# A cross-attention kernel in two-level Strassen form: GpSimd's reductions placed ahead of VectorE work on PSUM, one operand sum handed to DMA, one product in blocks in fewer batches

## The chip, the cores and the metric

The kernel runs on one core of a Trainium2 chip. The metric is the device time of one execution in microseconds (us); lower is better. The kernel before took 707.7 us, the median of three runs (703.13 to 709.08). A profile is one further execution, seen through the hardware profiler, with its own time.

The core has a matrix engine (TensorE, "PE" in the profile, with its weight loads as "PEld"), VectorE ("DVE"), ScalarE ("ACT"), GpSimd ("POOL") and SyncE ("SP"), each with an instruction queue worked in order. They meet only by semaphores. DMAs are issued from the queues of SP, ACT and POOL. TensorE writes to PSUM; VectorE and ScalarE reach both PSUM and SBUF.

## The reference

All of it is float32, with 8 batches, C = 512 channels, N = 1024 positions and D = 64:

```python
q = jnp.einsum('bcn,dc->bnd', x1, Wq) + bq
k = jnp.einsum('bcn,dc->bdn', x2, Wk) + bk[:, None]
v = jnp.einsum('bcn,dc->bdn', x2, Wv) + bv[:, None]
attn = jax.nn.softmax(jnp.einsum('bnd,bdm->bnm', q, k), axis=2)
return jnp.einsum('bcm,bnm->bcn', v, attn) + x1
```

Since the rows of `attn` sum to one, the result is Wv · (x2 · attnᵀ) + bv + x1, and so the kernel computes it: first Y = x2 · E with E the exponentials, not yet divided, then Y is divided by the sums, then Wv · Y.

## The kernel before

**Layout.** The scores are held with the key position m on the partitions, in two tiles per batch, `e[0]` and `e[1]`, one for each half h of the queries (512 columns). The softmax runs over m, which means over eight tiles (VectorE folds them, 128x1024 at a time, L249, then the two halves of what is left, L253) and then over the 128 partitions. That last step is GpSimd's `partition_all_reduce`: `highest` (L268) for the maxima, `total` (L272) for the sums. Both read from SBUF what `fold_halves` has just written. The sums then go to HBM and back to be inverted and spread (`invert` with a reciprocal on VectorE at L280, `spread` at L287).

**Seven products instead of eight.** Y is a product of 2 x 2 blocks in Winograd's form of Strassen's algorithm. The left blocks are `a["11"]` to `a["22"]` (x2 transposed, loaded by DMA) with the sums S1 to S4; the right blocks are those of E with the sums T1 to T4. The seven products are numbered 1, 2, 6, 7, 5, 3, 4 in the order in which TensorE does them. Wv · Y is done in the same way, with sums of the weights made once (`w["S1"]` and so on) and sums of Y.

**Two forms of a product of the first stage.** In the plain form (`multiply`, L391) it is 2 x 4 matmuls of 128x512 per product, each seen as two records. In batches 2 to 8 all seven products are done **in blocks**: the same algorithm once more, seven inner products of 2 matmuls of 128x256 (L458, again two records each), for which VectorE first makes inner sums: `inner_left` (four of 128x256, L431) and `inner_right` (one of 128x1024 at L447, two of 128x512 at L450 and L451). What TensorE leaves is put together by ScalarE copies (L467, L495) and by VectorE: `complete` (L501 on PSUM, L535 in SBUF) and `join` (L550, PSUM plus SBUF). Product 6 in blocks needs in addition `reseed`, which writes the joined result back to PSUM (L557) for product 5 to add to.

**Order.** The whole program is one schedule written out by hand (`manual_schedule`): the order of the calls in `period` is the order in each engine's queue. `weave` takes one step of each of several lists in turn. A period handles the first stage of one batch s, the scores of the next batch n (`scores_0`, `scores_and`), and the second stage of s (`second(1)` to `second(4)`), with loads for the batches after (nn, nnn). On TensorE a steady period runs: products 1 and 2, product 6, four score tiles and the next queries, products 5, 7, 3, four score tiles and the next keys, product 4, then the seven products with the weights. While product 2 runs, VectorE folds the sums of half 1, makes the inner sums of product 6, and `total(s, 1)` starts GpSimd as soon as the fold is done; two inner sums of product 6 are still to come then. `highest(n, 0)` comes at the end of `scores_0`, `highest(n, 1)` after the result of product 4 has been taken out by `evict_y(s, "21")`, and `total(n, 0)` near the end, ahead of `evict_o(s, "21")`.

**S4.** The left sum S4 is one VectorE instruction over SBUF (L109, `sum_a(s, "S4")`), written with the opposite sign; `evict_t3` (L567) adds accordingly. S1, S2 and S3 of later batches already come by DMA: a plain load and an accumulating DMA from GpSimd's queue (`begin_s1`/`end_s1`, `add_11`). GpSimd's queue issues every accumulating DMA of the kernel: T3 (`sum_t3`, L340), T4 (`copy_t4`, L334), the sums of the exponentials (`add_tile`, L645), the x1 blocks of the output (L590, L641).

**Batch numbers.** The title counts from 1. The code counts from 0 in `s.b`: batch 3 is `s.b == 2`. Batch 1 (`s.b == 0`) has a schedule of its own.

Of the kernel before, what the change touches and what calls it, by code (L numbers as in the profile page):

```python
# [16 lines left out]
def kernel(  # L17
# [47 lines left out]
    nc = tc.nc  # L65
# [36 lines left out]
    def left_sums(a, *ks):  # L102

        for k in ks:
            if k == "S3":
                nc.vector.tensor_tensor(a["21"], a["11"], a["21"], ALU.subtract)
                a["S3"] = a["21"]
            elif k == "S4":
                nc.vector.scalar_tensor_tensor(a[k], a["12"], -1.0, a["S2"], ALU.mult, ALU.subtract)  # L109
            else:  # L110
                x, y, op = {"S1": ("21", "22", ALU.add), "S2": ("11", "S1", ALU.subtract)}[k]
                nc.vector.tensor_tensor(a[k], a[x], a[y], op)
# [13 lines left out]
    class Batch:  # L126
        def __init__(self, b):
            self.b = b
            self.a, self.e, self.t, self.y, self.o = {}, {}, {}, {}, {}
            self.mx, self.top, self.den, self.few, self.rden, self.row = {}, {}, {}, {}, {}, {}  # L130
            self.tmp, self.bank = {}, {}
            self.inner = {}

# [24 lines left out]
    def end_s1(s):  # L158

        nc.gpsimd.dma_start(s.a["S1"], x2T[s.b, 1, 1], accum_op=ALU.add)  # L160

    def negate(s, k):
# [87 lines left out]

    def fold_halves(s, h, op):
        f = s.mx[h]
        nc.vector.tensor_tensor(f[:, 0, :], f[:, 0, :], f[:, 1, :], op)  # L253

    def folds(s, h, kind, op):

        return [lambda i=i: fold(s, h, i, kind, op) for i in range(1, MH)] + [lambda: fold_halves(s, h, op)]

# [7 lines left out]
    def highest(s, h):  # L266
        s.top[h] = sb.tile([P, H], F32, tag="top", name=f"top_{s.b}_{h}", bufs=2)
        nc.gpsimd.partition_all_reduce(s.top[h], s.mx[h][:, 0, :], P, ReduceOp.max)  # L268

    def total(s, h):  # L270
        s.den[h] = sb.tile([P, H], F32, tag="den", name=f"den_{s.b}_{h}", bufs=2)
        nc.gpsimd.partition_all_reduce(s.den[h], s.mx[h][:, 0, :], P, ReduceOp.add)  # L272
        s.few[h] = sb.tile([P, H // P], F32, tag="few", name=f"few_{s.b}_{h}", bufs=2)
        nc.gpsimd.dma_start(
            s.few[h], s.den[h][0:1, :].rearrange("o (p f) -> o p f", p=P)
        )
# [74 lines left out]
    def sum_e(s, *ks):  # L351
        weave(sums_e(s, *ks))
# [211 lines left out]
    def evict_t3(s):  # L564
        s.y["T3"] = y = sb.tile([P, 2, H], F32, tag="y12", name=f"yT3_{s.b}")
        for j in range(2):
            nc.vector.tensor_tensor(y[:, j, :], s.bank["a", j], s.tmp[7][:, j, :], ALU.add)  # L567

# [5 lines left out]
    RESULT = {"11": ("c", 1), "22": ("c", 5), "12": ("a", None), "21": ("c", 6)}  # L574

    def evict_y(s, k):

        bank, add = RESULT[k]
        s.y[k] = y = sb.tile([P, 2, H], F32, tag=f"y{k}", name=f"y{k}_{s.b}")
        for j in range(2):  # L580
            nc.vector.tensor_tensor(y[:, j, :], s.bank[bank, j], s.tmp[add][:, j, :], ALU.add)

# [206 lines left out]
    def period(s, n, nn, nnn):  # L789

        late = s.b >= 1

        def first(i):
# [19 lines left out]

        def scores_0(*rows):
            then = scores_and(n, 0, 1, "c", next_queries if nn else nothing)
            if late:
                reseed(s)
            weave(folds(n, 0, "max", ALU.max), *rows)
            highest(n, 0)
            return then  # L820
# [11 lines left out]
        if s.b == 0:  # L832
# [3 lines left out]
            sum_e(s, "T1", "T2")  # L836
            fold_halves(s, 0, ALU.add)
            total(s, 0)
# [10 lines left out]
            first(6)  # L849
            scores_0()  # L850
            weave(inner_left(s, 4, s.a["22"], "a12"), inner_right(s, 4, s.t["T4"], "eT2"))
            lefts_3 = inner_left(s, 3, s.a["S4"], "aI3")
# [13 lines left out]
        else:  # L866
            complete_1 = multiply_seeded(s, 1, "y11")
            weave(
                folds(s, 1, "sum", ALU.add),
                [nothing, complete_1] + inner_right(s, 6, s.t["T2"], "yT1", "yT2"),  # L870
                [nothing, nothing] + inner_left(s, 6, s.a["S2"], "i2"),
            )
            total(s, 1)
            invert(s, 0)
            hooks = {5: lambda: copy_u1(s, 0), 4: lambda: copy_u1(s, 1)}
# [3 lines left out]
            complete_2()  # L879
            evict_y(s, "11")  # L880
            sum_t4(s)
            hooks = {6: lambda: copy_t4(s, 0), 5: lambda: copy_t4(s, 2)}
            complete_6, *join_6 = multiply_joined(s, 6, "v", hooks)
            evict_q = None
            if n:
                weave(
                    inner_right(s, 5, s.t["T1"], "y21", "u1"),
                    inner_left(s, 7, s.a["S3"], "yT4"),
                    [nothing, lambda: sum_a(s, "S4")],
                )  # L890
                complete_6()
                weave(join_6)
                evict_q = scores_0(inner_left(s, 5, s.a["S1"], "i2"))
                rights_7 = inner_right(s, 7, s.t["T3"], "yT1", "yT2")
            else:
                weave(
                    inner_left(s, 5, s.a["S1"], "a11"),
                    inner_right(s, 5, s.t["T1"], "y21", "u1"),
                    inner_left(s, 7, s.a["S3"], "yT4"),
                )  # L900
                complete_6()
                weave(join_6)
                reseed(s)
                sum_e(s, "T3")
                rights_7 = inner_right(s, 7, s.t["T3"], "yT1", "yT2")
                rights_7.pop(0)()
                sum_a(s, "S4")
            spread(s, 0)
            shares(s, 1)
            weave(rights_7, inner_left(s, 3, s.a["S4"], "aI3"))  # L910
            complete_5, *join_5 = multiply_joined(s, 5, "r", {6: evict_q} if nn else {})
            complete_5()
            weave(join_5, inner_right(s, 3, s.t["22"], "eT1"))
# [40 lines left out]
        if s.b == 0:  # L954
            weave(tops)
            highest(n, 1)
        hooks = {}
# [12 lines left out]
        if nn:  # L970
            load_a(nn, "21", "22")
        evict_y(s, "21")
        lefts_1 = rights_2 = []
        if late and n:
            if nn:
                tops[2]()
            lefts_1 = inner_left(n, 1, n.a["11"], "i2")
            rights_2 = inner_right(n, 2, n.e[0][:, 1], "eT4")
# [4 lines left out]
        if late and n:  # L983
            if nn is None:
                weave(tops, lefts_1[1:])
                lefts_1 = []
            highest(n, 1)
            add_11(n, "S3")
            weave(rights_2, lefts_1[1:])
# [32 lines left out]
        if n:  # L1022
# [9 lines left out]
            weave(early)  # L1032
            fold_halves(n, 0, ALU.add)
            total(n, 0)
# [44 lines left out]
```

## Time and profile before

| | |
|---|---|
| median of three runs | 707.7 us |
| the three runs | 707.7, 703.13, 709.08 us |
| the profiled execution | 707.89 us, span 706.1 us |
| mean granted clock of TensorE | 0.985 |
| busy, share of the span | PE 96%, DVE 93%, ACT 49%, POOL 31% |

The span goes from the first instruction to the end of the last; what lies around it is 1.8 us here. A busy PE is a PE with a matmul in flight: the records overlap, so the spacing of their starts tells the rate, 0.43 us for 128x512 and 0.22 us for 128x256 at the full clock. In a timeline line the columns are start, length, engine, line of the code, operation, output and inputs, shapes and count, and in brackets the idle time before with what ended it. In the list of waits a line reads "engine, tile, line <- what it waited for: us in total, times, longest".

### The profile page before, as it was taken

What the parts mean: (1) busy time and instruction counts of PE and PEld (TensorE: products, weight loads), DVE (VectorE), ACT (ScalarE), POOL (GpSimd) and SP (SyncE); (2) the same over time, 40 slices, a digit from 0 to 9 for tenths busy, and PEclk for the clock granted to TensorE, in tenths of its full rate; (3) what the DMA queues carried; (4) which work ended last, traced back from release to release, by engine and by line L of the source; (5) the groups of instructions that cost most, each with busy time, mean ns of one, the idle gap of its engine ahead of it and who ended that gap; (6) DMA issues with size and microseconds to landing.
All of it is one profiled execution on the core that took longest, in us unless ns stands there. A gap on an engine that the chain in (4) does not pass through costs nothing.

```text
span 706.1 us, 7562 instructions
## 1 busy us (share of the span) xinstructions
PE 675.8 (96%) x2528; PEld 423.8 (60%) x2528; DVE 656.3 (93%) x853; ACT 348.5 (49%) x605; POOL 221.9 (31%) x182
## 2 busy tenths in 40 slices
PE   9999999799999999999999999989999989996997
PEld 5333555666557664658547575466754757465863
DVE  1999998999999999999999999999999999999984
ACT  2733455456455564464754555535555547443320
POOL 0133215520445114441144401753034621353000
PEclk9999999899999999999999999998999999999999
DMA  9666479794996929967499857988579772499103
GB/s 305 246 242 237 89 239 161 199 219 122 252 237 176 270 77 291 231 158 247 124 268 232 181 163 204 214 209 188 156 179 192 183 152 39 97 207 282 41 1 119
DMA packets 50774, 131.11 MB, mean 186 GB/s; under 512 B 5552, under 2 KB 7856, under 8 KB 50736
## 3 DMA queue, kind: packets, MB, share of 16 engines
q0 software_dynamic: 22464, 54.60, 42.3%
q1 hardware_dynamic: 27984, 75.64, 29.8%
q8 instruction: 20, 0.33, 0.2%
q10 hardware_dynamic: 288, 0.39, 0.2%
q14 instruction: 18, 0.15, 0.1%
HBM read 87.30 MB, written 16.81 MB: 147 GB/s over the span
## 4 chain that ended last, share of the span: by engine, by line
PE 57%; DVE 26%; DMA 8%; issue 5%; POOL 2%; ACT 1%; SPq 1%; DVEq 0%; POOLq 0%; ACTq 0%
PE ps_ya L458 8%; PE ps_oa L391 6%; PE ps_yc L458 5%; DMA sum<-e 5%; DVE aI L431 4%; PE ps_s L229 4%; DVE eT L315 4%; DVE sum L249 4%; PE ps_q L182 3%; PE ps_i3chain L458 3%; PE ps_oc L391 3%; PE ps_o L411 3%; PE ps_i5chain L458 3%; PE ps_i4chain L458 3%; PE ps_i7chain L458 3%
## 5 line engine op out<-in xcount | busy, mean ns | idle before, releaser
L272 POOL PARTITION_ALL_REDUCE den<-sum x16 | 55.1, 3446 | 80.1 <-DVE sum L253 75.2
L268 POOL PARTITION_ALL_REDUCE top<-max x16 | 39.2, 2450 | 122.6 <-DVE max L253 104.1
L302 DVE TENSOR_TENSOR e<-e,top 128x1024 f32<-128x1024 f32 x60 | 69.9, 1216 | 1.7 <-POOL top L268 1.7
L645 POOL DMA_DIRECT2D sum<-e x21 | 28.5, 1356 | 122.0 <-ACT sum L650 51.5
L306 ACT ACTIVATE e<-e 128x1024 f32<-128x1024 f32 x60 | 61.9, 1057 | 5.8 <-DVE e L302 5.2
L391 PE MATMUL ps_oa<-yT,w_S 128*128 128x512 f32 x128 | 57.5, 592 | 0.0
L391 PE MATMUL ps_oc<-yT,w 128*128 128x512 f32 x128 | 57.4, 592 | 0.0
L238 ACT COPY e<-ps_s 128x1024 f32<-128x1024 f32 x46 | 45.7, 1032 | 13.7 <-issue 7.8
L229 PE MATMUL ps_s<-q,k 64*128 64x512 f32 x188 | 47.3, 608 | 0.9 <-ACT q L671 0.8
L391 PEld LDWEIGHTS ps_oa<-yT,w_S 128*128 128x128 f32 x128 | 24.3, 190 | 30.6 <-issue 30.6
L391 PEld LDWEIGHTS ps_oc<-yT,w 128*128 128x128 f32 x128 | 24.3, 190 | 30.6 <-issue 29.4
L249 DVE TENSOR_TENSOR max<-max,e 128x1024 f32<-128x1024 f32 x30 | 36.6, 1220 | 0.5
L402 ACT COPY uo<-ps_oa 128x512 f32<-128x512 f32 x32 | 18.7, 585 | 35.1 <-PE ps_oa L391 35.1
L458 PE MATMUL ps_i6chain<-eI6yT,aI 128*128 128x256 f32 x56 | 19.0, 473 | 16.7 <-DVE aI L431 16.7
L431 DVE TENSOR_TENSOR aI<-aS 128x256 f32<-128x256 f32 x44 | 32.6, 741 | 0.0
L495 ACT COPY ps_ya<-ps_i1chain 128x256 f32<-128x256 f32 x28 | 10.0, 357 | 41.2 <-PE ps_i1chain L458 37.7
L229 PEld LDWEIGHTS ps_s<-q,k 64*128 64x128 f32 x188 | 16.7, 186 | 22.2 <-issue 15.4
L391 PE MATMUL ps_oa<-y,w_S 128*128 128x512 f32 (+1 forms) x68 | 28.8, 567 | 0.0
L391 PE MATMUL ps_o<-y,w 128*128 128x512 f32 x64 | 28.8, 592 | 0.0
L411 PE MATMUL ps_o<-y,w 128*128 128x512 f32 x64 | 28.8, 592 | 0.0
L572 DVE TENSOR_TENSOR y<-y,den 128x1024 f32<-128x1024 f32 x24 | 28.6, 1220 | 0.1
L431 DVE TENSOR_TENSOR aI<-a 128x256 f32<-128x256 f32 x58 | 27.5, 476 | 0.0
(217 smaller groups left out, 1698.7 us busy)
## 6 DMA issues: line engine op xcount, KB each, us to landing
x_in_x_dram<-in_x_dram SPq DMA_DIRECT2D x60, 512.0 KB, 6.0
a<-in_x2T_dram SPq DMA_DIRECT2D x32, 512.0 KB, 8.0
sum<-e POOLq DMA_DIRECT2D x21, 512.0 KB, 8.7
aS<-in_x2T_dram POOLq DMA_DIRECT2D x14, 512.0 KB, 8.0
uo<-in_x_dram POOLq DMA_DIRECT2D x14, 512.0 KB, 10.5
r<-in_x_dram POOLq DMA_DIRECT2D x14, 512.0 KB, 11.2
out_dram<-r SPq DMA_DIRECT2D x14, 512.0 KB, 4.7
eT<-eT POOLq DMA_DIRECT2D x14, 512.0 KB, 8.4
```

The source lines that it names most:

```text
L229: nc.tensor.matmul(ps[g], s.k[r, ts(i, P)], s.q[r, ts(h, H)], start=True, stop=True)
L238: nc.scalar.copy(e[:, :, i, :], whole)
L249: nc.vector.tensor_tensor(f, e[:, :, 0, :] if i == 1 else f, e[:, :, i, :], op)
L268: nc.gpsimd.partition_all_reduce(s.top[h], s.mx[h][:, 0, :], P, ReduceOp.max)
L272: nc.gpsimd.partition_all_reduce(s.den[h], s.mx[h][:, 0, :], P, ReduceOp.add)
L302: nc.vector.tensor_tensor(e, e, top, ALU.subtract)
L306: nc.scalar.activation(e, e, AF.Exp)
L391: nc.tensor.matmul(ps[:, n], left[ka][:, k, ts(j, P)], right[kb][:, k, n], start=opens and k == 0, stop=i in (2, 3, 4) and k == n_k - 1, s ...
L411: nc.tensor.matmul(ps, w["11"][:, k, ts(j, P)], s.y["11"][:, k, :], start=k == 0, stop=False, skip_group_check=True)
L431: return lambda: nc.vector.tensor_tensor(v[k], v[x], v[y], op)
L458: nc.tensor.matmul(ps, s.inner[i][ka][:, k, :], s.inner[i, "t"][kb][:, k, :], start=opens and k == 0, stop=z in (2, 3, 4) and k == MH // 2 ...
L572: nc.vector.tensor_tensor(s.y[k], s.y[k], rden, ALU.mult)
```

## The change

1. **`fold_halves` for sums** writes to a tile of its own, `half`, instead of in place; the last fold of the halves is taken out of the list that `folds` returns and is called by name. `total` now calls it itself.
2. **`total(s, 1)`** then comes after all inner sums of product 6, and what follows it on VectorE is `complete_2` and `evict_y(s, "11")`, both on PSUM. `invert(s, 0)`, which stood behind `total(s, 1)`, moves behind them.
3. **`highest(n, 0)`** moves from `scores_0` to behind the completion of product 5. `spread(s, 0)` and `shares(s, 1)` (GpSimd's DMAs and a reciprocal) stay behind it, and behind them `join_5` on PSUM.
4. **`highest(n, 1)`** of batches 2 to 6: the fold before it moves between the two halves of `evict_y(s, "21")`, which read PSUM.
5. **S4** of batches 2 to 8: a load from SyncE's queue (`begin_s4`) and an accumulating DMA from GpSimd's (`end_s4`) that adds S2. The sign turns, `evict_t3` subtracts. In batch 1 it stays a VectorE instruction.
6. **Product 6 in blocks** only where `six` holds: `s.b` 2, 3, 4, 5 and 7, which is batches 3 to 6 and 8. Batches 2 and 7 do it in the plain form, `first(6)`, without its inner sums, completion, joins and `reseed`. The order in which the inner sums of products 5, 7 and 3 are woven changes a little everywhere.

```diff
@@ left_sums @@
-            elif k == "S4":
-                nc.vector.scalar_tensor_tensor(a[k], a["12"], -1.0, a["S2"], ALU.mult, ALU.subtract)
             else:
-                x, y, op = {"S1": ("21", "22", ALU.add), "S2": ("11", "S1", ALU.subtract)}[k]
+                x, y, op = {
+                    "S1": ("21", "22", ALU.add),
+                    "S2": ("11", "S1", ALU.subtract),
+                    "S4": ("12", "S2", ALU.add),
+                }[k]
...
+    def begin_s4(s):
+
+        s.a["S4"] = sb.tile([P, MH, C // 2], F32, tag="aS4", name=f"aS4_{s.b}")
+        nc.sync.dma_start(s.a["S4"], x2T[s.b, 0, 1])
+
+    def end_s4(s):
+
+        nc.gpsimd.dma_start(s.a["S4"], s.a["S2"], accum_op=ALU.add)
...
     def fold_halves(s, h, op):
+
         f = s.mx[h]
-        nc.vector.tensor_tensor(f[:, 0, :], f[:, 0, :], f[:, 1, :], op)
+        s.half[h] = f[:, 0, :]
+        if op == ALU.add:
+            s.half[h] = sb.tile([P, H], F32, tag="top", name=f"half_{s.b}_{h}", bufs=2)
+        nc.vector.tensor_tensor(s.half[h], f[:, 0, :], f[:, 1, :], op)
 
     def folds(s, h, kind, op):
 
-        return [lambda i=i: fold(s, h, i, kind, op) for i in range(1, MH)] + [lambda: fold_halves(s, h, op)]
+        return [lambda i=i: fold(s, h, i, kind, op) for i in range(1, MH)]
...
     def total(s, h):
+        fold_halves(s, h, ALU.add)
...
     def evict_t3(s):
...
-            nc.vector.tensor_tensor(y[:, j, :], s.bank["a", j], s.tmp[7][:, j, :], ALU.add)
+            nc.vector.tensor_tensor(y[:, j, :], s.tmp[7][:, j, :], s.bank["a", j], ALU.subtract)
...
@@ period @@
         late = s.b >= 1
+        six = late and (n is None or s.b >= 2 and nn is not None)
...
             complete_1 = multiply_seeded(s, 1, "y11")
-            weave(
-                folds(s, 1, "sum", ALU.add),
-                [nothing, complete_1] + inner_right(s, 6, s.t["T2"], "yT1", "yT2"),
-                [nothing, nothing] + inner_left(s, 6, s.a["S2"], "i2"),
-            )
+            adds = folds(s, 1, "sum", ALU.add)
+            if six:
+                weave(
+                    adds,
+                    [nothing, complete_1] + inner_right(s, 6, s.t["T2"], "yT1", "yT2"),
+                    [nothing, nothing] + inner_left(s, 6, s.a["S2"], "i2"),
+                )
+            else:
+                weave(adds, [nothing, complete_1] + inner_left(s, 7, s.a["S3"], "yT4"))
             total(s, 1)
-            invert(s, 0)
...
             complete_2()
             evict_y(s, "11")
+            invert(s, 0)
+            begin_s4(s)
+            end_s4(s)
             sum_t4(s)
...
-                    [nothing, lambda: sum_a(s, "S4")],
...
-                evict_q = scores_0(inner_left(s, 5, s.a["S1"], "i2"))
...
+                if n:
+                    evict_q = scores_0()
+                    weave(inner_left(s, 5, s.a["S1"], "i2"))
+                    weave(folds(n, 0, "max", ALU.max))
+                else:
+                    reseed(s)
+                    sum_e(s, "T3")
             else:
...
+                copy_t4(s, 0)
+                copy_t4(s, 2)
+                first(6)
+                weave(inner_right(s, 5, s.t["T1"], "y21", "u1"), inner_left(s, 5, s.a["S1"], "i2"))
+                evict_q = scores_0()
+                weave(folds(n, 0, "max", ALU.max))
+            rights_7 = inner_right(s, 7, s.t["T3"], "yT1", "yT2")
+            weave(rights_7, [nothing, nothing] + inner_left(s, 3, s.a["S4"], "aI3"))
+            complete_5, *join_5 = multiply_joined(s, 5, "r", {6: evict_q} if nn else {})
+            complete_5()
+            if n:
+                fold_halves(n, 0, ALU.max)
+                highest(n, 0)
             spread(s, 0)
             shares(s, 1)
-            weave(rights_7, inner_left(s, 3, s.a["S4"], "aI3"))
-            complete_5, *join_5 = multiply_joined(s, 5, "r", {6: evict_q} if nn else {})
-            complete_5()
             weave(join_5, inner_right(s, 3, s.t["22"], "eT1"))
...
-        evict_y(s, "21")
+        if late and nn:
+            steps = evictions_y(s, "21")
+            steps[0]()
+            fold_halves(n, 1, ALU.max)
+            steps[1]()
+        else:
+            evict_y(s, "21")
```

`evictions_y` returns the two VectorE instructions of `evict_y` as a list. The remaining lines of the diff put the calls of `fold_halves` where the lists used to bring them.

## The prediction

> **What bounds the kernel.** I read the page's shares first: TensorE and VectorE are both nearly full, so the question is which of them waits for the other, and where.
>
> ```profile
> PE 675.8 (96%) x2528; PEld 423.8 (60%) x2528; DVE 656.3 (93%) x853; ACT 348.5 (49%) x605; POOL 221.9 (31%) x182
> ```
>
> The list of waits for TensorE and its weight loads has one large place, the inner products of product 6, waiting for VectorE's inner left sums (L431), once in each of batches 2 to 8:
>
> ```profile
> PE ps_i6chain L458 <- DVE aI L431: 16.7, 7, 3.4
> PEld ps_i6chain L458 <- issue: 19.3, 7, 3.8
> ```
>
> The timelines of batch 3 around it, TensorE, VectorE and GpSimd in turn, show why the sum is late:
>
> ```profile
> 220.71 1.03 PE L458 MATMUL ps_i6third<-eI6yT,aI 128*128 128x256 f32 x4
> 223.40 1.10 PE L458 MATMUL ps_i6chain<-eI6yT,aI 128*128 128x256 f32 x4 [1.67 <-DVE aI L431]
> ...
> 218.66 0.68 DVE L253 TENSOR_TENSOR sum<-sum 128x512 f32<-128x512 f32 x1
> 219.26 0.68 DVE L450 TENSOR_TENSOR eI6yT<-eI6yT,eT 128x512 f32<-128x512 f32 x1
> 219.86 2.46 DVE L431 TENSOR_TENSOR aI<-aS 128x256 f32<-128x256 f32 x1
> 222.25 0.68 DVE L451 TENSOR_TENSOR eI6yT<-eT,eI6yT 128x512 f32<-128x512 f32 x1
> 222.85 0.87 DVE L431 TENSOR_TENSOR aI<-aS,aI 128x256 f32<-128x256 f32 x2
> ...
> 219.44 3.59 POOL L272 PARTITION_ALL_REDUCE den<-sum  x1 [5.49 <-DVE sum L253]
> ```
>
> An inner sum that takes 0.41 us elsewhere takes 2.46 us beside GpSimd's reduction: VectorE is held for 2.05 us. Another reduction of the same batch begins ahead of work on PSUM:
>
> ```profile
> 209.64 1.40 DVE L637 SCALAR_TENSOR_TENSOR o<-ps_oc,bv_sb,uo 128x512 f32<-128x512 f32 x2
> 210.96 2.18 DVE L315 TENSOR_TENSOR eT<-eT,e 128x1024 f32<-128x1024 f32 x1
> ...
> 209.83 3.23 POOL L272 PARTITION_ALL_REDUCE den<-sum  x1 [3.14 <-DVE sum L253]
> ```
>
> The two instructions on PSUM keep their 0.74 us each; the SBUF one behind them (1.22 us undisturbed) ends at 213.14, as if released at about 212.0. So a sum holds VectorE's two-input SBUF work until about 2.2 us after its start. A maximum does so for about 1.0 us (237.55 to 238.55: the L447 instruction beside it takes 1.98 instead of 1.22).
>
> The rest of TensorE's time in batch 3 is matmul against matmul: successive starts show no other gap. So a period of 83.2 us is 81.4 us of TensorE and 1.83 us of product 6 waiting. In batches 2, 6 and 8 the wait reaches 3.3 to 3.6 us, and then the matmuls behind it come 0.43 us apart instead of 0.22:
>
> ```profile
> core 0: us, PE busy (x) PEld busy (x) DVE busy (x) ACT busy (x) POOL busy (x), PEclk, DMA share, GB/s
> 137.00:142.00 5.00, 3.87 (x9) 3.18 (x10) 4.93 (x11) 1.32 (x2) 3.81 (x6) 0.50 0.26 43
> ```
>
> The granted clock (PEclk) is 0.50 there, which costs another 2 to 3 us.
>
> **The change, part by part.**
>
> *Product 6, batches 3 to 6.* The fold (0.60) and the hold (2.05) go from in front of the inner sum S2 (the first of the last pair, ended at 223.2). It is then ready at 223.2 - 2.05 - 0.60 = 220.6. TensorE wants it at 220.71 + 0.86 = 221.57, so the wait goes, with 1.0 us to spare. Batches 3, 4, 5: 3 x 1.83 = 5.5 us. Batch 6 takes from 469.49 to 481.98 for product 6, 12.5 us, where gapless it takes 6.2 (28 starts at 0.216 and the change of stage): 6.3 us lost. Its VectorE was 1.5 us late, because one accumulation of sums took 12.2 us to land (427.24 to 439.48) instead of about 7.5. I leave a 0.3 us wait: 6.0.
>
> *Product 6 plain, batches 2 and 7.* 16 records at 0.429 us are 6.87 us against 6.05: 0.82 us more on TensorE, while VectorE is rid of one 128x1024, two 128x512 and four 128x256 sums, a completion and two joins (1.14 + 1.20 + 1.36 + 0.60 + 1.20 = 5.5 us). Its operands are on time: T2 ends at 127.8 in batch 2, S2 lands at 126.2, TensorE asks at 131.77. Batch 2 went from 131.77 to 144.81, 13.04 us; now 6.97: 6.1 saved. Batch 7 also waited 3.65 us in product 5 (568 to 574), since VectorE was behind. From 557.01 to the start of product 7 at 578.56 it took 21.55; plain product 6, scores and product 5 back to back are 6.97 + 3.55 + 6.15 = 16.67: 4.9 saved.
>
> *Batch 8* is bound by VectorE from 629.4, where the last accumulation lands, until product 6 is joined and reseeded (TensorE goes on at 653.84). Only the hold counts: 2.05 less what is left of it (below) = 1.5. TensorE then idles about as long in product 5 as it did in both places together.
>
> *Where the holds go.* Behind `total(s, 1)` come L501 and two L581 (0.60 + 1.20 us on PSUM) and the reciprocal, then an L447 on SBUF: of 2.2 us some 0.3 to 0.5 are left. `highest(n, 0)`: 0.6 us of `join_5` covers part of 1.0, and 0.5 is left of 0.76. `highest(n, 1)`: the fold ends 0.60 earlier, the second L581 covers 0.6, and the scaling of y21 behind it is held for 0.55, where 0.85 fell on an inner sum nobody was waiting for. That scaling ended at 273.04 and now ends at about 273.6, against `second(2)` at 273.80, which needs it. This is the tightest margin. Completion of product 4 waited for ScalarE at 266.09, so VectorE cannot run ahead there. I count 0.2 us in each of five batches: -1.0.
>
> The Trainium skill ("SBUF — State Buffer", Who interferes with whom) says that a VectorE instruction with two SBUF inputs and a GpSimd instruction that reads SBUF exclude each other, for the whole instruction. The first half the rows bear out, the second they don't: the record is 3.23 us, the hold 2.2. With a hold as long as the record, 1.4 instead of 0.4 us would be left after `total(s, 1)` and the y21 scaling would miss `second(2)` by up to 1.5 us: five batches, 7.5 us, a time near 692.
>
> *S4.* VectorE is rid of 1.22 us (L109, off TensorE's path once product 6 is on time: nothing by itself). In its place come a SyncE load and an accumulating DMA, two GpSimd queue entries' worth of order. In batch 3 the buffer is free at 220, when product 2 ends. The nearest rows:
>
> ```profile
> aS<-in_x2T_dram SPq DMA_DIRECT2D x7, 512.0 KB, 7.9
> sum<-e POOLq DMA_DIRECT2D x21, 512.0 KB, 8.7
> eT<-eT POOLq DMA_DIRECT2D x14, 512.0 KB, 8.4
> ```
>
> Loaded by 228, issued on GpSimd (1.3 us), added behind T3's two accumulations, which land about 2.7 us apart: S4 lands near 236, or at 239 if the loads of x2, which start at 235 now and at 233 then, slow it. (The DMA share is 0.34 from 219 to 227, and 1.06 from 227 to 235 while T3 and T4 are added.) GpSimd waits for the load with T4's accumulations, the row DMA of sums and the maximum behind it: T4 lands near 241 instead of 237.4 and is wanted at 255; the maximum is not ready to start before 241. VectorE reaches the sums of S4 near 238, TensorE needs S4 at 245.6. T3 is queued behind the later `total` and lands about 1.1 us later (233.1), just ahead of L447's need near 234.5. Cost of the two DMAs: between nothing and, at the longest landing seen (12.2 us each), S4 at 246; I take nothing, since the medians are four times nearer. The denominators go out some 4 us later and are back by 254 at worst, wanted at 257.
>
> *Plus or minus nothing:* the sign in `evict_t3` (same shape, 0.68), the separate `half` tile (its buffer is last read long before), S4 of batch 1 as an ordinary sum.
>
> **Sum.** 5.5 + 6.0 + 6.1 + 4.9 + 1.5 - 1.0 = 23.0 us off 707.9 (span 706.1 and 1.8 around it), which makes 685. The profiled time is the median. The run at 703.1 fits one without batch 6's late landing (4.4 us): it may be missing before, and costs little after.
>
> **Rivals.**
>
> 1. *Another thing is late (19%).* The accumulated sums of the exponentials landed only 1.3 us ahead of VectorE in batch 3, and behind it in batches 2, 6 and 8. If they, T3 or y21 make TensorE wait about 1.5 us in each of six batches, 9 us come back: 694. For it: the DMA queues carry 1 MB more each period. Against: S4 goes out while product 6 to 5 run, 40 us ahead of those sums, and VectorE gains 3 us a period.
> 2. *The PSUM work is held too (5%).* Then the change doesn't do what it says, and the 2.05 us fall on L501. The inner sums of product 6 are still out before it, so TensorE loses little: 687. Against: L637 at 0.74.
> 3. *Slower: S4 comes late (7%).* VectorE stands at the sums of S4 in order, with product 5's completion, the maximum and product 3's sums behind it. About 3 us of slack lie there. If S4 lands at 244 or later instead of 236, TensorE stands 3.4 us, or less with a clock drop, in each of seven batches, and the gain of 23 is gone; at 248 each batch loses near 7 with the drop: 710 to 735, say 720. For it: GpSimd's order, the DMA share of 1.06 and the 12.2 us landing. Against: the medians.
> 4. *No difference (3%):* the saved time turns up as waits in the second stage.
>
> **Chances.** Forecast 66%, 681 to 689. Faster by over 1% (about what a measurement of this kernel can tell): 0.66 + 0.19 + 0.05 = 0.90; same 0.03; slower 0.07. The range reaches down to 680 (batch 8 without its clock drop) and up to 695, which takes in rivals 1 and 2.
>
> **What would show it.** L431 at 0.42 beside every `total`, no wait of product 6 in batches 3 to 7, a period of 81.4 us, no granted clock of 0.5 but in batch 8; VectorE idle for 2 to 3 us a period. It would be wrong if TensorE waits at `second(2)` for y21, or product 3 for S4, or if the last accumulation lands later against product 6.

## The result, and the profile after

The kernel after takes 684.94 us (median of 4 runs, 684.15 to 686.32) against 705.41 us for the kernel before on the same chip (4 runs, 702.35 to 709.08). The ratio is 0.971, with a 95% interval from 0.965 to 0.977. The forecast was 685.0. The profiled execution took 684.92 us, with a span of 683.1 us and a mean granted clock of 0.997 (before: 707.89, 706.1 and 0.985).

The first part of the page of the kernel after, busy time and share of the span for each engine:

```profile
PE 669.0 (98%) x2504; PEld 415.0 (61%) x2504; DVE 625.4 (92%) x826; ACT 345.8 (51%) x595; POOL 217.7 (32%) x189
```

TensorE has 24 matmul records fewer and is busy 7 us less; VectorE is rid of 27 instructions and 31 us. Of the seven waits of product 6 (16.7 us in all) those of batches 2 to 7 are gone from TensorE's list of waits after. What is left of it, with the longest wait of product 5, lies in batch 8:

```profile
PE ps_i5chain L474 <- ACT d L483: 4.8, 1, 4.8
PE ps_i6third L474 <- DVE aI L447: 1.5, 1, 1.5
...
PE ps_i6chain L474 <- DVE aI L447: 0.8, 1, 0.8
```

The line numbers have moved: the inner left sum L431 is L447 now, the first inner right sum L447 is L463, and the completion L501 is L517. The timelines of batch 3 in the kernel after, TensorE, VectorE and GpSimd in turn, answer those shown of before:

```profile
215.05 1.03 PE L474 MATMUL ps_i6third<-eI6yT,aI 128*128 128x256 f32 x4
215.91 1.03 PE L474 MATMUL ps_i6chain<-eI6yT,aI 128*128 128x256 f32 x4
...
214.52 0.88 DVE L447 TENSOR_TENSOR aI<-aS,aI 128x256 f32<-128x256 f32 x2
215.32 0.68 DVE L268 TENSOR_TENSOR half<-sum 128x512 f32<-128x512 f32 x1
215.92 0.69 DVE L517 TENSOR_TENSOR ps_yc<-ps_yc,v 128x512 f32<-128x512 f32 x1
216.52 1.28 DVE L597 TENSOR_TENSOR y<-ps_yc,uy 128x512 f32<-128x512 f32 x2
217.72 0.16 DVE L296 RECIPROCAL few<-few 128x4 f32<-128x4 f32 x1
217.83 1.58 DVE L463 TENSOR_TENSOR eI5y<-eT 128x1024 f32<-128x1024 f32 x1
...
216.11 3.22 POOL L288 PARTITION_ALL_REDUCE den<-half  x1 [7.82 <-DVE half L268]
```

The second inner product (one line of four records) starts 0.86 us after the first, with no gap. The last inner sums of product 6 come before the fold now. Beside the reduction (216.11 to 219.33) the instructions on PSUM keep their lengths, 0.69 us and 1.28 for a pair, and the reciprocal takes 0.16; only the SBUF instruction behind them is long, 1.58 instead of 1.22. The 0.36 us too many say that it could run from 218.19: the hold ends 2.08 us after the reduction's start, though its record goes on to 3.22.

Cut by batches, from the start of one product 1 to the next (to the end of the span in batch 8), the 23 us are here; batch 1 has got 0.43 us longer:

| batch | before | after | gain | forecast |
|---|---|---|---|---|
| 2 | 88.08 | 81.99 | 6.09 | 6.1 |
| 3, 4, 5, each | 83.21 | 81.17 | 2.04 to 2.06 | 1.83 |
| 6 | 87.52 | 81.17 | 6.35 | 6.0 |
| 7 | 80.41 | 76.51 | 3.90 | 4.9 |
| 8 | 80.75 | 79.87 | 0.88 | 1.5 |
| y21, second(2) | | | 0 | -1.0 |
| sum, with batch 1 | | | 22.9 | 23.0 |

The half clock of batch 2 is gone with its wait. Windows of the kernel after, the first over the same stretch as before and the second over product 5 of batch 8, where TensorE restarts after 4.77 us:

```profile
core 0: us, PE busy (x) PEld busy (x) DVE busy (x) ACT busy (x) POOL busy (x), PEclk, DMA share, GB/s
137.00:142.00 5.00, 5.00 (x20) 2.11 (x20) 3.60 (x7) 2.19 (x4) 4.41 (x8) 1.00 0.69 176
...
632.00:640.00 8.00, 8.00 (x34) 6.85 (x33) 7.48 (x14) 2.00 (x6) 1.95 (x3) 0.86 1.05 191
```

### The profile page after: what moved, and what is told of

Same layout as the page of the kernel before. It is cut to its first block, busy times and chain, and to the rows that moved or that the text cites. A ratio compares the mean times of both kernels' runs of the same rounds, so it can differ in the third digit from the quotient of the medians.

```text
span 683.1 us, 7499 instructions
## 1 busy us (share of the span) xinstructions
PE 669.0 (98%) x2504; PEld 415.0 (61%) x2504; DVE 625.4 (92%) x826; ACT 345.8 (51%) x595; POOL 217.7 (32%) x189
## 4 chain that ended last, share of the span: by engine, by line
PE 93%; DVE 4%; DMA 1%; ACT 1%; issue 1%; SPq 0%; DVEq 0%; ACTq 0%
PE ps_oa L407 12%; PE ps_ya L474 10%; PE ps_oc L407 8%; PE ps_yc L474 8%; PE ps_s L240 6%; PE ps_ya L407 5%; PE ps_o L407 4%; PE ps_o L427 4%; PE ps_q L193 4%; PE ps_k L193 3%; PE ps_i4chain L474 3%; PE ps_i3chain L474 3%; PE ps_i5chain L474 3%; PE ps_i7chain L474 3%; PE ps_i1chain L474 3%; PE ps_i2chain L474 2%
## 5 line engine op out<-in xcount | busy, mean ns | idle before, releaser
L288 POOL PARTITION_ALL_REDUCE den<-half x16 | 51.6, 3225 | 91.2 <-DVE half L268 91.2
L283 POOL PARTITION_ALL_REDUCE top<-max x16 | 31.7, 1980 | 131.3 <-DVE few L296 58.2
L588 DVE TENSOR_TENSOR y<-y,den 128x1024 f32<-128x1024 f32 x24 | 30.4, 1293 | 0.3
L407 PE MATMUL ps_ya<-eT,aS 128*128 128x512 f32 x64 | 28.3, 595 | 0.0
L193 PE MATMUL ps_k<-x_in_x_dram,wqk_sb 128*64 128x512 f32 x112 | 26.0, 600 | 0.4 <-DMA x_in_x_dram<-in_x_dram 0.4
L331 DVE TENSOR_TENSOR eT<-eT,e 128x1024 f32<-128x1024 f32 x16 | 26.1, 1637 | 0.0
```

Of the source, the lines that this page charges most:

```text
L193: nc.tensor.matmul(ps[r, :], w_sb[:, c, :], s.x[:, c, ts(h, H)], start=(c == 0), stop=(c == CT - 1),)
L283: nc.gpsimd.partition_all_reduce(s.top[h], s.half[h], P, ReduceOp.max)
L288: nc.gpsimd.partition_all_reduce(s.den[h], s.half[h], P, ReduceOp.add)
L407: nc.tensor.matmul(ps[:, n], left[ka][:, k, ts(j, P)], right[kb][:, k, n], start=opens and k == 0, stop=i in (2, 3, 4) and k == n_k - 1, s ...
L588: nc.vector.tensor_tensor(s.y[k], s.y[k], rden, ALU.mult)
```

## The experiments

The kernel before took a median of 704 to 711 us in the different sets, so each experiment is read by its ratio to the before of its own set, and by its trace. Differences in us to the kernel after are between medians of different sets, and where they are small the traces decide.

### The place of the sum over the partitions

**e1: the sum of half 1 moved, nothing else.** From the kernel before:

```diff
-                folds(s, 1, "sum", ALU.add),
+                folds(s, 1, "sum", ALU.add)[:3],
...
+            fold_halves(s, 1, ALU.add)
             total(s, 1)
-            invert(s, 0)
...
             evict_y(s, "11")
+            invert(s, 0)
```

> The kernel before with one edit: the sum over the partitions of half 1 starts behind the inner sums of product 6 (fold in place, as before), and the reciprocal of half 0 behind the result of product 1. S4, the maxima and product 6 in blocks stay. Theory (product 6 waited for an inner sum that GpSimd's reduction held up): no wait of product 6 in batches 3 to 6, periods of 81.4 us; batch 2 keeps about 2 of its 7 us, batches 7 and 8 gain 1 to 1.7 each as VectorE bounds them: 688 to 691 us. Rival (VectorE is simply too full, and what counts is that S4 and two product-6 preparations leave it): 700 us or more.

Measured: 692.41 us, ratio 0.982 (0.979 to 0.985). That is 14.0 us of the 20.5 that the whole change brought in its own set. It is 1.4 us more than the top of what the theory gave, and far from the rival's 700. In batches 3 to 5 the wait of product 6 is gone, but a period is 81.47 us and not 81.17: product 5 takes 6.45 us to product 7 instead of 6.15. In batches 2 and 6 product 5 loses about 1 us, and in batch 7 it takes 12.36 us to product 7. In batches 2, 6 and 7 TensorE now waits for the inner left sums of product 5 (4.4 us in all), so VectorE is behind there. It has S4 and more inner sums to make than in the kernel after; which of them is to blame this run does not tell.

**e2: the sum of half 1 left out.** From the kernel before:

```diff
-        nc.gpsimd.partition_all_reduce(s.den[h], s.mx[h][:, 0, :], P, ReduceOp.add)
+        whole = s.b == 0 or h == 0
+        if whole:
+            nc.gpsimd.partition_all_reduce(s.den[h], s.mx[h][:, 0, :], P, ReduceOp.add)
...
-            s.few[h], s.den[h][0:1, :].rearrange("o (p f) -> o p f", p=P)
+            s.few[h], (s.den[h] if whole else s.mx[h][:, 0, :])[0:1, :].rearrange("o (p f) -> o p f", p=P)
```

> The kernel before without GpSimd's sum over the partitions of half 1 in batches 2 to 8 (the first partition's partial sums are taken as if they were the total, so half of each output is divided by the wrong numbers); the fold and the inner sums stay in their old order. Theory: the inner sum takes 0.42 instead of 2.46 us, is ready 0.4 us before TensorE asks, and the wait of 1.83 us goes: 687 to 691 us. Rival (the place of the fold among the inner sums is what delays them, not the reduction): the wait stays at 1.2 us or more, 700 us or more.

Measured: 689.98 us, ratio 0.979 (0.975 to 0.982). The fold is still in its old place, ahead of the inner sums, and without the reduction the wait of product 6 is gone in batches 3 to 6 (periods of 81.17 to 81.27 us). The timelines of batch 3 of this kernel, TensorE and VectorE (L433 is L431 of the kernel before):

```profile
217.71 1.03 PE L460 MATMUL ps_i6chain<-eI6yT,aI 128*128 128x256 f32 x4
...
216.00 0.42 DVE L433 TENSOR_TENSOR aI<-aS 128x256 f32<-128x256 f32 x1
```

The inner sum that took 2.46 us takes 0.42. So it was the reduction that made product 6 wait; the 0.60 us of the fold alone do not.

**e3: the sum of half 1 put back early, in the kernel after.**

```diff
-            adds = folds(s, 1, "sum", ALU.add)
+            adds = folds(s, 1, "sum", ALU.add) + [lambda: total(s, 1)]
...
-            total(s, 1)
```

> The changed kernel with the fold and the sum of half 1 back in their old place among the inner sums. Theory: the inner sum for product 6 comes 2.65 us later, 1.0 us were to spare, so 1.7 us of waiting return in each of batches 3 to 6 and some 1.2 in batch 8, nothing in batches 2 and 7 where product 6 is plain: 692 to 694 us. Rival (VectorE has enough room now without S4): 685 to 687 us.

Measured: 692.36 us, ratio 0.981 (0.978 to 0.985). The old picture is back in batch 3; the timelines of this kernel, TensorE, VectorE, GpSimd:

```profile
217.10 1.10 PE L474 MATMUL ps_i6chain<-eI6yT,aI 128*128 128x256 f32 x4 [1.67 <-DVE aI L447]
...
213.55 2.47 DVE L447 TENSOR_TENSOR aI<-aS 128x256 f32<-128x256 f32 x1
...
213.14 3.59 POOL L288 PARTITION_ALL_REDUCE den<-half  x1 [5.49 <-DVE half L268]
```

An inner sum of 0.42 us takes 2.47, TensorE stands 1.67 us, and a period is 83.08 us. Batch 8 loses 1.4. Batches 2 and 7 lose nothing, because in the plain form no inner sum of product 6 stands behind the reduction. The same edit is worth 14.0 us in the kernel before (e1) and 7.4 here. By the traces the difference lies in batches 2 and 6: it gains 3.8 and 4.8 us there, and nothing and 1.9 here. In batch 2 the two edits remove the same wait.

### Product 6 plain

**e6: product 6 in blocks in batches 2 and 7 too.** From the kernel after:

```diff
-        six = late and (n is None or s.b >= 2 and nn is not None)
+        six = late
```

> The changed kernel with product 6 in blocks in batches 2 and 7 as well. Theory: 0.82 us of TensorE saved twice, against waits of 1 + 1.7 us in batch 2, whose last accumulation lands late, and 1 to 3 us in batch 7, where VectorE bounds product 5: 686 to 689 us. Rival (the plain form is the larger part of the gain, as the batches' own gains of 6.1 and 3.9 us suggest): 693 to 696 us.

Measured: 686.88 us, ratio 0.973 (0.968 to 0.978), 1.9 us above the kernel after. Batch 2 goes from 81.99 to 83.38 us and batch 7 from 76.51 to 77.51. So of the 6.1 and 3.9 us that these batches gained, the plain form itself gives 1.4 and 1.0 once the other edits are there; the rest those edits give without it.

### The maxima

**e5: both maxima in their old places.** From the kernel after:

```diff
-                    weave(inner_left(s, 5, s.a["S1"], "i2"))
-                    weave(folds(n, 0, "max", ALU.max))
+                    weave(
+                        folds(n, 0, "max", ALU.max) + [lambda: fold_halves(n, 0, ALU.max)],
+                        inner_left(s, 5, s.a["S1"], "i2"),
+                    )
+                    highest(n, 0)
...
+                fold_halves(n, 0, ALU.max)
+                highest(n, 0)
...
-            if n:
-                fold_halves(n, 0, ALU.max)
-                highest(n, 0)
...
-            steps = evictions_y(s, "21")
-            steps[0]()
+            evict_y(s, "21")
             fold_halves(n, 1, ALU.max)
-            steps[1]()
```

> The changed kernel with both maxima over the partitions back in their old places (half 0 straight behind its folds, half 1 behind both parts of the result of product 4). Theory (TensorE sets the period; the holds of 0.8 us each fall on sums nobody waits for): 684.5 to 686 us. Rival (each hold of VectorE is paid): 0.5 us twice in six batches, 690 us.

Measured: 685.64 us, ratio 0.971 (0.967 to 0.975). The difference of 0.7 us to the kernel after is within what the runs tell apart. The maxima hold VectorE for a shorter time than the sums, and in batches 2 to 6 their old places cost TensorE nothing that the trace shows. (Batch 5 of the profiled execution is 1.0 us longer, but there VectorE stood 1.20 us for an accumulating DMA.) Batch 7 is 0.4 us longer, between the scores and product 4. The timelines of the kernel after show what is left of their holds, VectorE, TensorE and GpSimd:

```profile
235.22 1.63 DVE L463 TENSOR_TENSOR eI3eT<-e 128x1024 f32<-128x1024 f32 x1
...
264.32 1.58 DVE L588 TENSOR_TENSOR y<-y,den 128x1024 f32<-128x1024 f32 x1
...
266.10 1.45 PE L407 MATMUL ps_o<-y,w 128*128 128x512 f32 x3
...
234.74 1.78 POOL L283 PARTITION_ALL_REDUCE top<-max  x1 [9.56 <-DVE few L296]
...
263.78 1.78 POOL L283 PARTITION_ALL_REDUCE top<-max  x1 [2.45 <-DVE max L268]
```

Against 1.22 us undisturbed, the two SBUF instructions are 0.41 and 0.36 us too long, so the holds end 0.89 and 0.90 us after the reductions' starts. The scaling of y21 ends at 265.90, and `second(2)` starts at 266.10 without a wait.

### S4 by DMA

**e4: S4 on VectorE again.** From the kernel after:

```diff
-            begin_s4(s)
-            end_s4(s)
...
+                    [nothing, lambda: sum_a(s, "S4")],
...
```

> The changed kernel with S4 made by VectorE again (one sum of 128x1024 in each of batches 2 to 8, woven into the inner sums of product 5 as before), no DMAs for it. Theory (TensorE sets the period, VectorE has 2 to 3 us of room): 685 to 686.5 us, the one possible loss being 1.1 us in batch 8, which VectorE bounds. Rival (VectorE sets the period): 1.2 us in each of seven batches, 693 us.

Measured: 689.07 us, ratio 0.977 (0.974 to 0.980): neither the theory's 685 to 686.5 nor the rival's 693. Product 6 still waits for nothing in batches 2 to 6. The loss is in the scores' second half: from its first tile to product 4 it takes 7.75 us instead of 7.22 in batches 3 to 5 and 8.08 in batch 6, and batch 8 is 0.84 us longer: 3.3 us by these, of 3.4 in the spans. Of the kernel with S4 on VectorE, the tile of scores on bank a (its list of what it waited for: us, times), then the timelines of TensorE's weight loads and of VectorE:

```profile
  DVE yT L583: 4.1, 10
...
247.61 0.35 PEld L240 LDWEIGHTS ps_sa<-q,k 64*128 64x128 f32 x2 [0.50 <-DVE yT L583]
248.21 0.18 PEld L240 LDWEIGHTS ps_sa<-q,k 64*128 64x128 f32 x1 [0.24 <-DVE yT L583]
...
246.88 1.27 DVE L583 TENSOR_TENSOR yT<-uy,ps_ya 128x512 f32<-128x512 f32 x2
```

The same in the kernel after, where the list has 0.7 us, and the weight loads run through:

```profile
  DVE yT L583: 0.7, 2
...
247.26 0.62 PEld L240 LDWEIGHTS ps_sa<-q,k 64*128 64x128 f32 x4 [0.23 <-issue]
...
245.53 0.70 DVE L517 TENSOR_TENSOR ps_ya<-ps_ya,v 128x512 f32<-128x512 f32 x1 [0.42 <-ACT ps_ya L511]
246.14 1.28 DVE L583 TENSOR_TENSOR yT<-uy,ps_ya 128x512 f32<-128x512 f32 x2
```

The subtraction of `evict_t3` (L583) takes the result of product 3 out of bank a of PSUM, in two halves, and a score tile is written to bank a next. In the kernel after VectorE has 0.42 us of idle time ahead of it. The first half of the bank is free at 246.82, 0.44 us before the tile's weights are loaded at 247.26, and the second half at 247.42, 0.27 us before its weights at 247.69. So there is room for some 0.9 us ahead of the first half and 0.7 ahead of the second. The 1.21 us of S4 are more than that; what is over comes to 0.3 to 0.5 us, and the period loses 0.53. VectorE is not short of time over the whole period: later in the same batch of e4 it still stands idle for 0.36 and 0.75 us.

**e10: the same, with the score tile on bank a put last** instead of third. From e4:

```diff
-            scores_and(n, 1, 2, "a", nothing)
+            scores_and(n, 1, 3 if s.b else 2, "a", nothing)
```

> The kernel after with S4 on VectorE again, and of the scores' second halves the tile on bank a put last instead of third (batches 2 to 7). Theory: what S4 on VectorE cost (689.07 against about 685 us) is that the subtraction that empties bank a comes some 0.8 us later and the score tile on bank a waits for it; with that tile one place (0.86 us) later the wait for this reason is gone from the list of waits. The tile that takes its place waits for ScalarE's copy of an earlier tile instead, an estimated 0.35 us, so the time is 686 to 688.5 us. Rival: VectorE is simply short of 0.5 us in every period, the wait turns up at another instruction on VectorE's results, and the time stays at 689 us or above.

Measured: 689.25 us, ratio 0.968 (0.965 to 0.972). By the time, which is that of e4, it is the rival that came true. By the trace, the wait for bank a is gone from its list, as the theory had it, and in its place TensorE waits for ScalarE's copy of an earlier tile. The timeline of TensorE in batch 3 of this kernel:

```profile
248.48 1.13 PE L240 MATMUL ps_s<-q,k 64*128 64x512 f32 x4 [0.26 <-ACT e L249]
```

The step between two starts is 0.84 us there instead of 0.43. The run alone cannot tell what would have happened without that new wait.

**e11: that order of the tiles alone,** in the kernel after with S4 by DMA. The diff is that of e10.

> The kernel after with S4 by DMA, as it is, and only the order of the score tiles changed as in the run before: the tile on bank a last instead of third. It prices that order by itself. Theory (what S4 on VectorE cost is the wait for bank a, and with the other order the same time went to the wait for ScalarE's copy): that order alone costs the 0.41 us of ScalarE's wait in each of batches 2 to 7, scores to product 4 takes about 7.6 to 7.75 instead of 7.22 us, and the time is 687 to 688.5 us. Rival (the order costs nothing, and VectorE was short of 0.5 us wherever the tile stood): 685 to 685.7 us.

Measured: 687.12 us, ratio 0.975 (0.972 to 0.978), as the theory had it. The order costs 7.74 us from scores to product 4 in place of 7.22 by itself. With it, the periods of batches 3 to 6 are 81.69 or 81.70 us whether S4 is on VectorE (e10) or comes by DMA (e11); of the 1.75 us between the two spans 1.2 are in batch 8 and 0.5 ahead of batch 2. So in a period that ScalarE makes 0.5 us longer, S4 on VectorE costs nothing more. This does not show that bank a was the only place short of time, since the longer period gives VectorE more room everywhere; for bank a speak the waits in the trace of e4.

**e8: S4's accumulating DMA behind T4's two** on GpSimd's queue. From the kernel after:

```diff
             begin_s4(s)
-            end_s4(s)
             sum_t4(s)
...
+                end_s4(s)
                 complete_6()
                 weave(join_6)
...
                 copy_t4(s, 0)
                 copy_t4(s, 2)
+                end_s4(s)
                 first(6)
```

> The changed kernel with the accumulating DMA of S4 issued behind the two of T4 on GpSimd's queue instead of ahead of them. In batch 3 S4 then lands near 239 instead of 230.5 us, where VectorE asks at 231.8 and TensorE at 239.7. Theory (there are about 3 us of slack behind VectorE's wait, as the prediction reckoned): product 3 waits 3 to 4 us for its inner sums in each of batches 2 to 7, with a half clock behind some: 703 to 718 us. Rival (the DMA has ample room): 685 to 688 us.

Measured: 719.11 us, ratio 1.018 (1.014 to 1.023), slower than before and just above what the theory gave. Its timelines in batch 3, VectorE and TensorE:

```profile
243.94 0.76 DVE L447 TENSOR_TENSOR aI<-aS 128x256 f32<-128x256 f32 x2 [6.97 <-DMA aS<-aS]
...
249.19 2.05 PE L474 MATMUL ps_i3third<-eI3eT,aI 128*128 128x256 f32 x4 [3.32 <-DVE eI3eT L463]
251.02 1.91 PE L474 MATMUL ps_i3chain<-eI3eT,aI 128*128 128x256 f32 x4
```

S4 lands at 243.92; measured from product 1 of the batch that is 8.3 us later than in the kernel after. VectorE stands 6.97 us, TensorE 3.32, and then an inner product of four records takes 1.7 to 1.8 us from start to start instead of 0.86. The batch is 87.79 us long, 6.6 more than after: half for the wait and half for the slower clock of TensorE.

### Batch 8

**e7: product 6 plain in batch 8 too.** From the kernel after:

```diff
-        six = late and (n is None or s.b >= 2 and nn is not None)
+        six = s.b >= 2 and nn is not None
...
-                evict_q = scores_0()
-                weave(folds(n, 0, "max", ALU.max))
+                if n:
+                    evict_q = scores_0()
+                    weave(folds(n, 0, "max", ALU.max))
+                else:
+                    sum_e(s, "T3")
```

> The changed kernel with product 6 plain in batch 8 too. Theory: batch 8 has no more waiting for inner sums of product 6 (1.7 + 0.9 us), for the reseeding (4.9 us), nor the half clock behind it (1 us), and pays 0.82 us: product 7 starts 8 us earlier, 676 to 679 us. Rival (batch 8 is bound by VectorE or by the loads of x1 and S4 anyway, and the wait comes back in products 7 to 4): 682 to 686 us.

Measured: 682.96 us, ratio 0.967 (0.963 to 0.971), as the rival had it. Product 7 starts 8.5 us earlier after product 1, and then product 3 waits for S4. Its timelines, VectorE and TensorE:

```profile
636.25 0.76 DVE L447 TENSOR_TENSOR aI<-aS 128x256 f32<-128x256 f32 x2 [6.60 <-DMA aS<-aS]
...
640.47 1.62 PE L474 MATMUL ps_i3third<-eI3eT,aI 128*128 128x256 f32 x4 [3.08 <-DVE eI3eT L463]
```

The load of S4 stands behind four loads of x1 on SyncE's queue: issued at 621.17 and landed at 630.70, where in batch 3 of the kernel after it took 3.6 us.

**e9: the loads of x1 behind that of S4.** From e7:

```diff
-        if n is None:
-            load_x(s, x1)
...
             begin_s4(s)
+            if n is None:
+                load_x(s, x1)
             end_s4(s)
```

> The kernel with product 6 plain in batch 8 too, and in batch 8 the four loads of x1 issued behind the load of S4 instead of ahead of it. Theory: in the run before this one the load of S4 stood behind four loads of x1 on SyncE's queue (issued 621.17, landed 630.70 us) and product 3 waited 1.27 + 3.24 us for S4, at half clock behind that; with the load first, S4 lands some 4 to 9 us earlier, product 3 waits for nothing, and the time is 676 to 678 us. Rival: VectorE, or the x1 blocks that come later now, bound batch 8 all the same, and the time stays at 681 to 683 us, with the wait of product 3 moved to another instruction.

Measured: 679.76 us, ratio 0.955 (0.951 to 0.959) to a before that took 711.24 in this set; batch 8 is 75.34 us instead of 77.95 in e7. The time lies between the two expectations. The load landed 6.1 us earlier, at 624.60, but the accumulation, issued at 625.18, took 7.9 us more. VectorE stood 3.61 us for it, and TensorE still waits. Its timeline of TensorE:

```profile
637.37 1.10 PE L474 MATMUL ps_i3third<-eI3eT,aI 128*128 128x256 f32 x4 [1.67 <-DVE eI3eT L463]
```

**e12: S4 of batch 8 alone on VectorE,** where it had stood idle. From e7, with the loads of x1 in the place of S4's:

```diff
-        if n is None:
-            load_x(s, x1)
...
-            begin_s4(s)
-            end_s4(s)
+            if n:
+                begin_s4(s)
+                end_s4(s)
+            else:
+                load_x(s, x1)
...
             rights_7 = inner_right(s, 7, s.t["T3"], "yT1", "yT2")
+            if n is None:
+                weave(rights_7)
+                rights_7 = []
+                sum_a(s, "S4")
```

> Product 6 plain in batch 8 too, and S4 of batch 8 alone on VectorE, behind the inner sums of product 7, where VectorE had stood 3.61 us for the DMA (629.54 to 633.15 us); S4 of batches 2 to 7 by DMA. Theory: the sums of S4 begin 2.4 us earlier, the inner sum of e that product 3 waited 1.83 us for (637.14) is ready at about 634.8, ahead of TensorE, which asks at 635.5, the half clock behind goes too, and the time is 676 to 677.5 us. Rival: the DMA was not what made batch 8 late, another operand of product 3 comes no earlier, and the time stays at 679 to 681 us.

Measured: 677.03 us (676.69 to 677.29), ratio 0.961 (0.957 to 0.964) to a before of 703.95, and the fastest kernel of this study: 7.9 us below the kernel after. Its timelines, VectorE and TensorE:

```profile
628.73 1.22 DVE L114 TENSOR_TENSOR aS<-a,aS 128x1024 f32<-128x1024 f32 x1
...
632.85 1.22 DVE L463 TENSOR_TENSOR eI3eT<-e 128x1024 f32<-128x1024 f32 x1
...
634.83 1.03 PE L474 MATMUL ps_i3third<-eI3eT,aI 128*128 128x256 f32 x4
```

The sum of 1.22 us takes the place of 3.61 us of waiting, the operand of product 3 is ready at 634.07, and TensorE asks at 634.83. Batch 8 is 72.2 us long, and the mean granted clock of the execution is 1.000.

## Why the prediction was right

**The wait of product 6** was the reduction's hold on VectorE, and both sides of that were shown: it goes when the reduction is moved (e1) or left out (e2), and comes back with it (e3). Batches 3 to 5 gave 2.05 us each instead of 1.83; of the rest, 0.13 us is product 5, which got shorter too: the prediction had seen no gap there.

**Batches 2 and 6** were sized within 0.4 us. What the prediction put down to the plain form in batch 2, though, belongs mostly to no edit alone: the moved sum by itself gains 3.8 of the 6.1 us (e1), the change without the plain form 4.7 (e6), and the change without the moved sum all of them (e3).

**Batch 7** was sized too high, by 1.0 us. The sum took product 6, scores and product 5 to run back to back in 16.67 us; they took 17.37, since product 5 starts 0.66 us late, behind ScalarE's copy of the scores. It did so in the kernel before too: 4.21 us from the scores to product 5 in both, where the sum has 3.55. The stretch from scores to product 4 is 0.54 us longer than before, and product 4 is 0.24 shorter. Part of that stretch is the wait that e4 shows in other batches: both waits for L583 in the list after, 0.7 us, lie in batch 7.

**Batch 8** gave 0.9 for 1.5 us. The last accumulation landed 0.7 us later after product 1 than in the kernel before, which was on the prediction's list of what would make it wrong. The prediction's reading of batch 8 held, that VectorE bounds it and the wait mostly moves: product 6 waits 2.3 us instead of 4.3, and product 5 4.77 instead of 2.06.

**The wait of `second(2)` for y21** (-1.0 us) did not come. Its margin was named as the tightest, at 0.2 us, and is 0.20 in the trace, so by its own times no wait was due and the 1.0 us were a reserve; the hold left on the scaling was 0.36 us instead of 0.55.

**That the sum met the time to 0.1 us is luck.** Batches 3 to 6 gave 1.0 us more than forecast and the reserve for y21 was not used, another 1.0; batches 7 and 8 gave 1.6 less, and batch 1 lost 0.4. And 23 us is the step between the two profiled executions: the medians of the set are 20.5 us apart.

**S4 off VectorE, "nothing by itself"** is the step that was wrong, although the sum does not show it. The runs make it 3.4 us in the spans and 4.1 in the medians (e4). The reason given was that S4 leaves TensorE's path once product 6 is on time, and the prediction saw VectorE idle for 2 to 3 us a period. VectorE does stand idle for 2.3 us in each of batches 3 to 6. But its room counts from one place to the next: ahead of `evict_t3` it was 0.7 to 0.9 us, and S4 takes 1.21. The forecast of gapless periods was right only because this edit was in the change.

**S4's landing** was sized well. Batch 3 starts 5.66 us earlier in the profile after; with these added, S4's load lands at 223.7 (forecast 228), S4 at 236.1 (forecast 236), VectorE asks for it at 237.4 (238) and TensorE at 245.4 (245.6). Here are lines of the page after on DMA issues, with the median us from issue to landing as the last number:

```profile
aS<-in_x2T_dram SPq DMA_DIRECT2D x14, 512.0 KB, 6.3
...
eT<-eT POOLq DMA_DIRECT2D x14, 512.0 KB, 12.1
...
aS<-aS POOLq DMA_DIRECT2D x7, 512.0 KB, 8.6
```

T4 pays for S4 ahead of it on the queue, 12.1 us for 8.4 (8.4 in e4 too, where S4 is not a DMA), and lands at 244.7 instead of 241, still well ahead of its use at 253. The margin of S4 on VectorE is 1.3 us.

**The rivals.** PSUM work is not held: 0.69 us, and 1.28 for a pair, beside the reduction. S4 late was a real danger, and its price of 720 us was right (e8: 719), for a landing 8.3 us later. The point from which it decides was too rough: for a landing at 244 the prediction had 3.4 us a batch, "or less with a clock drop", and at about 244.5 the run has 6.6. Something else late did not come except in batch 8, at 0.7 us.

**The rule weighed** was that of the Trainium skill, "SBUF — State Buffer", sections "SBUF: two separate sides" and "Who interferes with whom": that the exclusion of VectorE's and GpSimd's SBUF work lasts for the whole instruction. For this reduction it does not, as far as GpSimd's record tells its end. VectorE goes on 2.08 us after the start of a sum with a record of 3.22 us, and 0.90 us after that of a maximum with a record of 1.78. (The prediction's 2.2 us was read a little high: its row gives 213.14 - 1.22 - 209.83 = 2.09.) The time is 685 and not the 692 that the rule would have made.

## What to carry to other kernels

Where a reduction on GpSimd shuts VectorE out of SBUF, put in front of it all that another engine is waiting for, and behind it work on PSUM; find the length of the hold from an instruction that outlasts it, not from the reduction's record. Work taken off a nearly full engine is worth what is missing at the next place where another engine waits for it, so look for the release of a PSUM bank as well as for operands. Put a transfer in place of an instruction only where the landing comes well before its use, and take the instruction back where the engine would stand waiting for the transfer, as in the last batch here.

## What the runs showed of the hardware that was not expected

**The exclusion goes both ways.** In batch 5 of the kernel before, a maximum took 5.25 us; the two shown of the kernel after took 1.78. Its timelines, VectorE and GpSimd:

```profile
440.94 1.22 DVE L447 TENSOR_TENSOR eI2eT<-e 128x1024 f32<-128x1024 f32 x1
442.08 0.42 DVE L431 TENSOR_TENSOR aI<-a 128x256 f32<-128x256 f32 x1
442.41 0.68 DVE L450 TENSOR_TENSOR eI2eT<-eI2eT,e 128x512 f32<-128x512 f32 x1
...
446.05 2.36 DVE L302 TENSOR_TENSOR e<-e,top 128x1024 f32<-128x1024 f32 x2 [1.68 <-POOL top L268]
...
440.77 5.25 POOL L268 PARTITION_ALL_REDUCE top<-max  x1
```

VectorE's SBUF instructions, back to back until 444.37, keep their lengths, and the reduction ends 1.65 us after the last of them, while VectorE waits 1.68 us for it. By these rows whichever is in keeps the other out. The sum at 219.44 in the prediction's lines fits this: it began while VectorE's L450 was under way, and its record is 3.59 us instead of 3.23. That the maximum was kept out from its first microsecond is read from the records; no run here tested it.

**TensorE's clock after a gap is not told by the gap's length alone.** A wait of 1.67 us in batch 3 of e3 was followed by matmuls 0.22 us apart, and one of 1.67 us in batch 8 of e9 by some that came 0.43 apart, with a granted clock of 0.76 from 640 to 645 us. In e8 five waits of 14.6 us together, 3.3 at most, cost product 3 25.1 us, so the clock was slow behind them too; the granted clock was 0.75 from 243 to 254 us. What else decides stays open.
